# An attention kernel's first and last microseconds: 24 drains ahead of VectorE's program, the sums checked before the last finishing steps, the last store from ScalarE's queue

## The chip, the cores and the metric

The kernel runs on one core of a Trainium2 chip. The metric is the device time of one execution in microseconds. Before the change it is 1798.63 us, the median of three runs (1798.06 to 1798.91).

## The reference

The input `x` has 32 images of 256 channels and 32 x 32 positions. It is group-normalised in 32 groups, projected to queries, keys and values, and goes through attention with 8 heads of 32 channels over the 1024 positions. A position attends only to earlier ones (`tril(..., -1)`); the first one attends to nothing. The result is added to `x`.

```
q, k, v = heads(q_w @ gn(x) + q_b), heads(kv_w @ gn(x) + kv_b)
scores  = where(mask == 0, -10000, q @ k.T / sqrt(32))
attn    = where(mask == 0, 0, softmax(scores))
out     = x + heads_back(attn @ v)
```

## The kernel before

The kernel is one long, unrolled program for each engine, `unshifted()`, followed by a fallback, `shifted()`, under a runtime condition. The first takes the exponentials of the scores without taking their maximum off; the fallback does the same work with the maximum taken off, in loops, and is there for inputs whose sums of exponentials leave the range from 1e-20 to 1e20. With the inputs of this case it is never entered.

In `unshifted()` the order on every engine is written out by hand (`tc.manual_schedule`). The work is cut into visits, 12 for an image and 384 in all. In a visit TensorE computes scores (line 310), products of exponentials and values (line 421) and projections for the next image (line 169); ScalarE takes the exponentials (lines 392 and 396); GpSimd masks the diagonal blocks (line 338); VectorE adds exponentials up over the keys (line 439). Sums of one image are folded by DMAs, inverted and used in `finish` some visits later: `finish` multiplies the products by the inverse sums (line 543), adds the bias of the values and `x` (line 545) and sends the result from SyncE's queue (line 551).

At the start VectorE takes statistics of the first image (line 184). They feed the first products of TensorE that are not mere warming up (line 169), and so everything behind them.

The last image has no later visits to hide in. Its sums are made by TensorE (line 473), inverted by `invert_here` (lines 530 to 533), and its last quarter is finished in `end_last`, in two halves of 256 columns. For each half VectorE transposes the sums, inverts them and spreads them (`invert_here`); then for each half it runs `finish`, whose store goes out as soon as the half is done. Behind that `end_last` looks whether all sums were in range:

```
check(inv_last.rearrange("p n k -> p (n k)"), 1.0 / SUM_MAX, 1.0 / SUM_MIN)
nc.vector.tensor_reduce(worst, in_range, AX.X, ALU.min)
nc.tensor.matmul(pc[0:1, 0:1], lhsT=worst, rhs=ones, start=True, stop=True)
nc.vector.tensor_scalar(outside, pc[0:1, 0:1], -1.0, float(P), ALU.mult, ALU.add)
```

`check` is lines 494 and 495, the reduction line 567, the matmul line 569 and the last VectorE step line 571. The number `outside`, rows that were out of range, is then loaded into a register of each of the five engines (line 901), with an assertion on SyncE that it lies from 0 to 128. Each engine compares it with zero and jumps over its part of `shifted()` (line 902), which lies in its program between the branch and the end. At the end SyncE waits for one semaphore after another, those of all DMA queues and engines (line 925; called its ladder below, each wait a rung), and a barrier of all engines closes the program.

Of the kernel before, what the change touches and what calls it, by code (L numbers as in the profile page):

```python
# [10 lines left out]
I32 = mybir.dt.int32  # L11
AF = mybir.ActivationFunctionType
ALU = mybir.AluOpType
# [4 lines left out]
P = 128  # L18
HD = 32
CPG = 8  # L20
HALF = 512
# [11 lines left out]
def tile_norm_attention_residual(  # L33
# [19 lines left out]
    nc = tc.nc  # L53
    B, C, H, W = x.shape
# [7 lines left out]
    const = ctx.enter_context(tc.tile_pool(name="const", bufs=1))  # L62

    x_in = x.rearrange("b (g p) h w -> b p g (h w)", p=P)
    x_out = out.rearrange("b (g p) h w -> b p g (h w)", p=P)
# [15 lines left out]
        out=avg, in_=avg, pattern=[[-CPG, P // CPG], [0, CPG]],  # L81
# [3 lines left out]
        out=avg, in_=avg, pattern=[[CPG, P // CPG], [0, CPG]],  # L85
# [13 lines left out]
    def unshifted():  # L99
# [9 lines left out]
        def load(b):  # L109
            width = S if b else HALF  # L110
            for g in range(NG):
                for at in range(0, S, width):
                    load_part(b, g, slice(at, at + width))
# [12 lines left out]
        def misc(name):  # L126
            return ps_m.tile([P, HALF], F32, tag="misc", name=name)


        def load_weights(junk):  # L130

            arrived = tc.alloc_semaphore("arrived")
            nc.scalar.activation(junk, live["x", 0][:, 0, HALF : HALF + 1], AF.Identity)
            nc.scalar.sem_inc(arrived, 1)
            nc.sync.wait_ge(arrived, 1)
            for n, w in enumerate((q_w, kv_w[0:C], kv_w[C : 2 * C])):
                live["wn", n] = epool.tile([P, 4, HALFBANK], F32, tag="eh", bufs=3, name=f"wn_{n}")[:, :NG, :C]
                nc.sync.dma_start(out=live["wn", n], in_=w.rearrange("(o p) c -> p o c", p=P))
            nc.sync.dma_start(out=qk_bias[:, 0, :], in_=q_b.rearrange("(g p) -> p g", p=P))
            nc.sync.dma_start(out=qk_bias[:, 1, :], in_=kv_b[0:C].rearrange("(g p) -> p g", p=P))  # L140
            nc.sync.dma_start(out=v_bias_col, in_=kv_b[C : 2 * C].rearrange("(g p) -> p g", p=P))
# [32 lines left out]
        def blocks(tokens, s, turned=False):  # L174

            of = tokens.rearrange("p (n s t) -> p n s t", s=2, t=P)[:, :, s, :]
            return of[:, :, ::-1] if turned else of
# [315 lines left out]
        def check(rows, least, most):  # L493
            nc.vector.scalar_tensor_tensor(in_range, rows, least, in_range, ALU.is_ge, ALU.mult)
            nc.vector.scalar_tensor_tensor(in_range, rows, most, in_range, ALU.is_le, ALU.mult)
# [27 lines left out]
        def invert_here(b, n, within=slice(0, HALF)):  # L523


            if ("rb", b) not in live:
                live["rb", b] = work.tile([P, 4, HALF], F32, tag="folded", bufs=1, name="rb_last")
            k = (within.stop - within.start) // HD
            turned = small.tile([P, HALF], F32, tag="turned", bufs=1, name=f"turned_{b}_{n}_{within.start}")[:, : k * HD]
            nc.vector.transpose(turned, live["den", n][:, within])  # L530
            inv = inv_last[:, n, within.start // HD : within.stop // HD]
            nc.vector.reciprocal(inv, turned.rearrange("p (k r) -> p k r", r=HD)[:, :, 0])
            nc.vector.transpose(  # L533
                live["rb", b][:, n, within].rearrange("p (k r) -> p k r", r=HD),
                inv.unsqueeze(2).broadcast_to([P, k, HD]),
            )

        def finish(b, n, within=slice(0, HALF), later=None):
            g, hf = divmod(n, NH)
            cols = slice(hf * HALF + within.start, hf * HALF + within.stop)  # L540
            num, rb, xt = live["num", b, n], live["rb", b][:, n, within], live["x", b]
            num = num[:, within]
            nc.vector.tensor_mul(num, num, rb)  # L543
            for s in range(2):
                nc.vector.scalar_tensor_tensor(  # L545
                    blocks(rb, s), blocks(num, s, s == 1), v_bias_col[:, g : g + 1], blocks(xt[:, g, cols], s),
                    ALU.add, ALU.add,
                )
            if cols.start == 0:
                nc.vector.tensor_copy(rb[:, 0:1], xt[:, g, 0:1])  # L550
            send = lambda: nc.sync.dma_start(out=x_out[b, :, g, cols], in_=rb)
            if later is None:
                send()
            else:
                later(send)

        def end_last(b):

            both = [slice(c * HALFBANK, (c + 1) * HALFBANK) for c in range(2)]
            for part in both:  # L560
                invert_here(b, 3, part)
            for part in both:
                finish(b, 3, part)

            check(inv_last.rearrange("p n k -> p (n k)"), 1.0 / SUM_MAX, 1.0 / SUM_MIN)
            worst = const.tile([P, 1], F32, name="worst")
            nc.vector.tensor_reduce(worst, in_range, AX.X, ALU.min)
            pc = misc("pc")
            nc.tensor.matmul(pc[0:1, 0:1], lhsT=worst, rhs=ones, start=True, stop=True)
            outside = const.tile([1, 1], I32, name="outside")  # L570
            nc.vector.tensor_scalar(outside, pc[0:1, 0:1], -1.0, float(P), ALU.mult, ALU.add)
            return outside

# [53 lines left out]
        def when(i, f, where=at):  # L629
            where.setdefault(i, []).append(f)  # L630
# [19 lines left out]
        SPREAD = (2, 2, 3, 4)  # L650
        FINISH = (N + 13, N + 13, N + 14, N + 16)
        every = range(4)

        with tc.manual_schedule(engines={ENG.PE, ENG.Activation, ENG.DVE, ENG.Pool, ENG.SP}):

# [1 line left out]
            junk = small.tile([P, 1], F32, tag="most", name="junk")  # L657
            nc.scalar.activation(junk, ones, AF.Exp)
            load_weights(junk)
            if B > 1:  # L660
                load(1)
            keep_busy(16)
# [30 lines left out]
            for b in range(B):  # L693
# [4 lines left out]
                if b >= 2:  # L698
                    for n in range(NG * NH):
                        cols = slice(n % NH * HALF, (n % NH + 1) * HALF)  # L700
# [5 lines left out]
                if not last:  # L706
# [16 lines left out]
                    for n in every:  # L723
                        v = first + (N + 9 + n // 2 if late else FINISH[n])
                        later = None if late else lambda send, first=first, v=v, n=n: when(*((first + 2 * N + 4, send) if n < 2 else (v + 1, send, after)))
                        when(v, lambda b=b, n=n, later=later: finish(b, n, later=later), after)
                else:
                    when(first + 3, lambda: sums(0, SUMMED[1], False), after)
                    when(first + 7, lambda: sums(1, SUMMED[5], False), after)
                    when(first + 9, lambda: sums(2, SUMMED[7], False), after)  # L730
                    when(first + 8, lambda b=b: invert_here(b, 0))
                    when(first + 9, lambda b=b: finish(b, 0))
                    when(first + 8, lambda b=b: invert_here(b, 1))
                    when(first + 8, lambda b=b: finish(b, 1))
                    when(first + 10, lambda b=b: invert_here(b, 2))
                    when(first + 11, lambda b=b: finish(b, 2), after)
            for i in range(B * N + 1):
# [4 lines left out]
                b, v = divmod(i - 1, N)  # L742
# [12 lines left out]
                for f in after.pop(i, ()):  # L755
                    f()
            assert not at and not between and not after
            outside = end_last(B - 1)
        for p in reversed(pools):
            p.release()  # L760
        for ins in nc.cur_bb.bb.instructions:
            if "TilePoolBoundary op=release" in ins.concise():
                tc.declare_no_dep(ins, group="first", reason="exponentials behind them are waited for")
        return outside

    def shifted():


        with ExitStack() as inner:
# [34 lines left out]
            with tc.For_i(0, B, 1) as b:  # L804
# [92 lines left out]
                    out=x_out[bass.ds(b, 1)].rearrange("o p g s -> p (o g) s"), in_=y.rearrange("p (g s) -> p g s", g=NG)  # L897
                )

    outside = unshifted()  # L900
    again = nc.values_load(outside[0:1, 0:1], min_val=0, max_val=P)
    with tc.If(again > 0):
        shifted()


# [23 lines left out]
```

## Time and profile before

| | us |
|---|---|
| median of three runs | 1798.63 |
| the profiled execution | 1799.27 |
| its span | 1797.57 |
| TensorE busy in the span | 1784.9 |
| VectorE busy | 1674.2 |
| ScalarE busy | 1456.0 |
| GpSimd busy | 879.7 |

In the profile PE is TensorE, DVE VectorE, ACT ScalarE, POOL GpSimd and SP SyncE. A q behind the name means the engine's sequencer, which also issues its DMAs. L551 is line 551 of the kernel before. Times in a timeline count from the start of the span. The granted clock of TensorE is 0.998 of full speed. Loading a register, branching, waiting for semaphores and issuing DMAs do not count as busy time, and the chain of work that the page follows back from the end starts at the last instruction that does.

### The profile page before, as it was taken

Reading aid. Unit: us, or ns where it says so; the run is one execution under the profiler, and the core shown is the slowest. Engines: PE = TensorE matmul, PEld = TensorE weight load, DVE = VectorE, ACT = ScalarE, POOL = GpSimd, SP = SyncE. Lnnn points to the kernel's source line nnn. Section 1 sums busy time; section 2 is a strip of 40 time slices with the busy share of each in tenths; the row PEclk is TensorE's granted clock in tenths of the full one; section 3 lists DMA queues with packets and bytes.
Section 4 is the critical chain, followed back from the end, with each engine's and each line's share of the span. In section 5 each row is a group of like instructions: output and inputs, shape, how many; then the busy total and the mean of one; then the engine's idle time right before and its main releaser. Section 6 shows DMA issues by size and latency. Waiting matters only on the chain.

```text
span 1797.6 us, 81793 instructions
## 1 busy us (share of the span) xinstructions
PE 1784.9 (99%) x37036; PEld 948.4 (53%) x37036; DVE 1674.2 (93%) x1830; ACT 1456.0 (81%) x1986; POOL 879.7 (49%) x902
## 2 busy tenths in 40 slices
PE   9999999999999999999999999999999999999997
PEld 5555555555555555555555555555555555555553
DVE  4689999999999999999999999999999999999998
ACT  6888878888778888788887888887888878888774
POOL 2345554554545455445545455554454544554541
PEclk9999999999999999999999999999999999999999
DMA  2566766766667667677676777666766666776663
GB/s 69 105 121 132 134 132 129 149 141 138 125 130 149 145 131 133 133 136 146 137 138 130 126 147 146 133 134 133 141 143 134 134 133 127 150 141 140 121 118 88
DMA packets 86819, 236.77 MB, mean 132 GB/s; under 512 B 21313, under 2 KB 22337, under 8 KB 70593
## 3 DMA queue, kind: packets, MB, share of 16 engines
q0 software_dynamic: 15872, 97.53, 39.8%
q1 hardware_dynamic: 70592, 133.96, 25.7%
q8 instruction: 290, 4.75, 1.2%
q14 instruction: 65, 0.52, 0.1%
HBM read 66.85 MB, written 34.57 MB: 56 GB/s over the span
## 4 chain that ended last, share of the span: by engine, by line
PE 99%; DVE 0%; ACT 0%; issue 0%; POOL 0%; POOLq 0%
PE sT L310 31%; PE acc L421 28%; PE pp L169 26%; PE ppv L169 13%; PE pd L473 1%; PE busy L155 0%; ACT e L396 0%; PE pv L169 0%; PE pm L169 0%; DVE rb_last L545 0%; PE wt L148 0%; ACT eh L392 0%; DVE rb_last L533 0%; DVE turned L530 0%; DVE acc L543 0%
## 5 line engine op out<-in xcount | busy, mean ns | idle before, releaser
L338 POOL TENSOR_SCALAR_AFFINE_SELECT diagonal<-eh 128x512 f32<-128x512 f32 x512 | 633.4, 1260 | 842.0 <-ACT eh L392 841.6
L396 ACT ACTIVATE e<-sT 128x1024 f32<-128x1024 f32 x768 | 744.3, 1022 | 249.8 <-PE sT L310 227.2
L439 DVE TENSOR_TENSOR e<-e,e 128x1024 f32<-128x1024 f32 x314 | 575.3, 1832 | 24.5 <-ACT v L274 3.2
L310 PE MATMUL sT<-q,k 32*64 32x128 f32 (+2 forms) x18432 | 579.4, 372 | 0.3 <-issue 0.2
L310 PEld LDWEIGHTS sT<-q,k 32*64 32x64 f32 x18432 | 395.0, 131 | 189.3 <-PE sT L310 69.6
L169 PE MATMUL pp<-xn,wT 128*32 128x512 f32 x4096 | 492.3, 598 | 0.0
L421 PE MATMUL acc<-e,v 128*32 128x512 f32 (+3 forms) x4608 | 401.0, 450 | 0.0
L392 ACT ACTIVATE eh<-sT 128x768 f32<-128x768 f32 (+1 forms) x384 | 341.7, 890 | 0.0
L421 PEld LDWEIGHTS acc<-e,v 128*32 128x32 f32 x4608 | 149.2, 110 | 261.5 <-issue 238.9
L169 PE MATMUL ppv<-wT,xn 128*32 128x256 f32 x4096 | 247.5, 382 | 0.0
L439 DVE TENSOR_TENSOR diagonal<-diagonal,e 128x1536 f32<-128x1536 f32 x126 | 195.1, 1548 | 17.1 <-PE acc L421 9.2
L169 PEld LDWEIGHTS pp<-xn,wT 128*32 128x32 f32 x4096 | 107.1, 109 | 195.8 <-issue 164.0
L439 DVE TENSOR_TENSOR e<-e,eh 128x1024 f32<-128x1024 f32 x126 | 163.9, 1301 | 6.5
L421 PEld LDWEIGHTS acc<-diagonal,v 128*32 128x32 f32 x4096 | 121.1, 110 | 87.6 <-issue 75.7
L439 DVE TENSOR_TENSOR e<-e,diagonal 128x2048 f32<-128x2048 f32 x63 | 144.2, 2289 | 19.3 <-POOL diagonal L338 19.2
L169 PEld LDWEIGHTS ppv<-wT,xn 128*32 128x32 f32 x4096 | 120.1, 109 | 79.7 <-issue 7.0
L421 PE MATMUL acc<-diagonal,v 128*32 128x128 f32 x4096 | 158.8, 273 | 0.0
L243 ACT ACTIVATE xn<-x,shift,rstd 128x256 f32<-128x256 f32 x248 | 136.8, 608 | 1.0 <-POOL shift L226 0.9
L543 DVE TENSOR_TENSOR num<-num,rb 128x512 f32<-128x512 f32 x124 | 122.8, 991 | 0.4 <-DMA rb<-inverses 0.4
L545 DVE SCALAR_TENSOR_TENSOR rb<-num,v_bias_col,x 128x256 f32<-128x256 f32 x248 | 117.5, 515 | 4.4
L452 POOL DMA_DIRECT2D e<-e x124 | 102.1, 823 | 38.6 <-issue 38.6
L452 POOL DMA_DIRECT2D diagonal<-diagonal x124 | 103.2, 832 | 5.8 <-issue 4.9
(80 smaller groups left out, 983.8 us busy)
## 6 DMA issues: line engine op xcount, KB each, us to landing
x<-in_x_dram SPq DMA_DIRECT2D x124, 256.0 KB, 3.7
diagonal<-diagonal POOLq DMA_DIRECT2D x62, 512.0 KB, 5.6
e<-e POOLq DMA_DIRECT2D x62, 512.0 KB, 6.1
rb<-inverses SPq DMA_DIRECT2D x124, 256.0 KB, 4.3
out_dram<-rb SPq DMA_DIRECT2D x124, 256.0 KB, 4.9
diagonal<-diagonal POOLq DMA_DIRECT2D x62, 256.0 KB, 4.6
folded<-diagonal SPq DMA_DIRECT2D x62, 256.0 KB, 5.3
e<-e POOLq DMA_DIRECT2D x62, 256.0 KB, 5.0
```

Source lines behind the costliest of these rows:

```text
L169: nc.tensor.matmul(out[part], lhsT=lhsT[:, part], rhs=rhs, start=start, stop=stop, skip_group_check=True)
L243: nc.scalar.activation(to, of, AF.Identity, bias=live["shift", b][:, g : g + 1], scale=rstd)
L310: return nc.tensor.matmul(bank[c : c + KEYS, cols], lhsT=live["k", b, g][rows, kb * P + c : kb * P + c + KEYS], rhs=live["q", b, g][rows, ...
L338: nc.gpsimd.affine_select(out=square[:, :, place + s * P : place + (s + 1) * P], in_=raw[:, :, (1 - s) * KEYS : (3 - s) * KEYS], pattern=[ ...
L392: exp = nc.scalar.activation(eh.rearrange("p (n bank) q -> p bank n q", n=2)[:, :, :, :narrow], short[:, :, :, :narrow], AF.Exp)
L396: nc.scalar.activation(e[:, 2 * a : 2 * a + 2, :wide], pairs[a][:, :, :wide], AF.Exp)
L421: nc.tensor.matmul(acc[HD * j : HD * (j + 1), of], lhsT=live["v", b][:, kb, h * HD : (h + 1) * HD], rhs=e[:, j, :], start=first, stop=last ...
L439: nc.vector.tensor_add(to, to, tile_of(b, g, at))
L452: nc.gpsimd.dma_start(out=total[:rows], in_=total[rows : 2 * rows], accum_op=ALU.add)
L473: nc.tensor.matmul(pd[HD * j : HD * (j + 1), of], lhsT=pick, rhs=e[:, j, :], start=start, stop=stop, skip_group_check=True,)
L543: nc.vector.tensor_mul(num, num, rb)
L545: nc.vector.scalar_tensor_tensor(blocks(rb, s), blocks(num, s, s == 1), v_bias_col[:, g : g + 1], blocks(xt[:, g, cols], s), ALU.add, ALU.add,
```

## The change

- Ahead of its first instruction of `unshifted()`, VectorE's program gets 24 drains, which wait until the engine has nothing in flight and do nothing else.
- In `end_last`, `check`, the reduction and the matmul come before both calls of `finish` instead of behind them.
- The count is no longer made from the matmul's result by VectorE (128 minus it): ScalarE copies the result itself into an integer, `inside`, the number of rows in range. The condition becomes `rows < P` instead of `again > 0`.
- The store of the second half is sent from ScalarE's queue, that of the first half from SyncE's as before.
- The assertion on the loaded value is left out.

```
-        def finish(b, n, within=slice(0, HALF), later=None):
+        def finish(b, n, within=slice(0, HALF), later=None, queue=nc.sync):
...
-            send = lambda: nc.sync.dma_start(out=x_out[b, :, g, cols], in_=rb)
+            send = lambda: queue.dma_start(out=x_out[b, :, g, cols], in_=rb)
...
                 invert_here(b, 3, part)
-            for part in both:
-                finish(b, 3, part)
-
             check(inv_last.rearrange("p n k -> p (n k)"), 1.0 / SUM_MAX, 1.0 / SUM_MIN)
...
             nc.tensor.matmul(pc[0:1, 0:1], lhsT=worst, rhs=ones, start=True, stop=True)
-            outside = const.tile([1, 1], I32, name="outside")
-            nc.vector.tensor_scalar(outside, pc[0:1, 0:1], -1.0, float(P), ALU.mult, ALU.add)
-            return outside
+            inside = const.tile([1, 1], I32, name="inside")
+            nc.scalar.copy(inside, pc[0:1, 0:1])
+            for part in both:
+                finish(b, 3, part, queue=nc.sync if part.start == 0 else nc.scalar)
+            return inside
...
+        ALIGN = 24
...
             load_weights(junk)
+            for _ in range(ALIGN):
+                nc.vector.drain()
...
-    again = nc.values_load(outside[0:1, 0:1], min_val=0, max_val=P)
-    with tc.If(again > 0):
+    rows = nc.values_load(
+        inside[0:1, 0:1], min_val=0, max_val=P, skip_runtime_bounds_check_because="it counts rows of one tile"
+    )
+    with tc.If(rows < P):
         shifted()
```

More of the change, by code (lines that the diff above doesn't have):

```diff
@@ L757, in unshifted @@
             assert not at and not between and not after
-            outside = end_last(B - 1)
+            inside = end_last(B - 1)
         for p in reversed(pools):
@@ L763, in unshifted @@
                 tc.declare_no_dep(ins, group="first", reason="exponentials behind them are waited for")
-        return outside
+        return inside
     def shifted():
@@ L898, in shifted @@
                 )
-    outside = unshifted()
-    again = nc.values_load(outside[0:1, 0:1], min_val=0, max_val=P)
-    with tc.If(again > 0):
+    inside = unshifted()
+    rows = nc.values_load(
+        inside[0:1, 0:1], min_val=0, max_val=P, skip_runtime_bounds_check_because="it counts rows of one tile"
+    )
+    with tc.If(rows < P):
         shifted()
```

## The prediction

> **What bounds the kernel now.** I read the page first: the row of busy times and the chain that ended last.
>
> ```profile
> PE 1784.9 (99%) x37036; PEld 948.4 (53%) x37036; DVE 1674.2 (93%) x1830; ACT 1456.0 (81%) x1986; POOL 879.7 (49%) x902
> ...
> PE 99%; DVE 0%; ACT 0%; issue 0%; POOL 0%; POOLq 0%
> ```
>
> TensorE is the bound, and the change leaves its 37,036 matmuls in place and in order. So only the two ends, where TensorE isn't the bound, can move. The second view is VectorE's timeline of the last 12 us (start, duration, what; idle time before it in brackets).
>
> ```profile
> 1787.98 0.45 DVE L533 STREAM_TRANSPOSE rb_last<-inv_last 128x256 f32<-128x256 f32 x1
> 1788.35 0.40 DVE L543 TENSOR_TENSOR acc<-acc,rb_last 128x256 f32<-128x256 f32 x1
> 1788.79 0.61 DVE L545 SCALAR_TENSOR_TENSOR rb_last<-acc,v_bias_col,x 128x128 f32<-128x128 f32 x2
> 1789.43 0.43 DVE L543 TENSOR_TENSOR acc<-acc,rb_last 128x256 f32<-128x256 f32 x1
> 1789.90 0.61 DVE L545 SCALAR_TENSOR_TENSOR rb_last<-acc,v_bias_col,x 128x128 f32<-128x128 f32 x2
> 1790.43 0.21 DVE L494 SCALAR_TENSOR_TENSOR in_range<-inv_last,in_range 128x64 f32<-128x64 f32 x1
> ...
> 1790.94 0.22 DVE L567 TENSOR_REDUCE worst<-in_range 128x1 f32<-128x64 f32 x1
> 1791.53 0.15 DVE L571 TENSOR_SCALAR outside<-pc 1x1 int32<-1x1 f32 x1 [0.37 <-PE pc L569]
> ```
>
> The last arithmetic ends at 1791.68, yet the span ends at 1797.57: 5.9 us hold no work at all, and the page's chain stops before them. The third view, the instructions of line 902 (the `If`), shows who is late there (durations in ns, then first start in us).
>
> ```profile
> L902 ACTq COMPARE_BRANCH  x1: 50/50/50, 1792.2 to 1792.2; - x1
> L902 POOLq COMPARE_BRANCH  x1: 45/45/45, 1792.3 to 1792.3; - x1
> ...
> L902 DVEq COMPARE_BRANCH  x1: 72/72/72, 1792.3 to 1792.3; - x1
> ...
> L902 ACTq EVENT_SEMAPHORE  x1: 17/17/17, 1792.7 to 1792.7; - x1
> ...
> L902 POOLq EVENT_SEMAPHORE  x1: 17/17/17, 1792.8 to 1792.8; - x1
> L902 DVEq EVENT_SEMAPHORE  x1: 21/21/21, 1796.5 to 1796.5; - x1
> ```
>
> Every engine jumps over the unused `shifted()`. ScalarE and GpSimd go on 0.4 us after their branch; VectorE goes on at 1796.47, 4.07 us after its branch ended at 1792.40, with nothing else to wait for. SyncE, which collects all semaphores before the last barrier, stands still for it; this is from its own waits (us in total, times, longest):
>
> ```profile
> SPq L925 <- DVEq L902: 2.6, 1, 2.6
> ```
>
> From there to the end it is 1.05 us (1796.52 to 1797.57).
>
> **Why VectorE is late.** The page's DMA queues show how instructions come in.
>
> ```profile
> q8 instruction: 290, 4.75, 1.2%
> q14 instruction: 65, 0.52, 0.1%
> ```
>
> Queue 14 brings 8 KB a packet. In the trace's records one such packet starts each time VectorE has begun 63 to 66 instructions more than a multiple of 128: at 341.79 us it stood at 447, at 429.01 at 578, at 603.48 at 832, at 1719.87 at 2497. So a page is 128 instructions, and crossing into one fetches the next. VectorE's last page began at about 2497 and ended at 2624; the fetched next one ended at about 2752. Its branch is its 2616th record, and the built program skips 137 instructions on VectorE, so the jump lands at 2754, just past both pages. For ScalarE (pages at 61 past a multiple of 128, branch 2725, 131 skipped) and SyncE (80 past, 1071, 126) the same count lands inside, and these were the quick ones.
>
> [...]
>
> **The change, part by part.** All on the profiled execution, 1799.27 us with a span of 1797.57; its 1.7 us around the span I leave alone. The median of the runs is 0.64 lower, and the same difference is taken from it.
>
> *The pad.* 24 drains added, one VectorE instruction (L571) gone: the branch is its 2639th record, in the page that starts near 2625; the target, 2777, lies in the next one (2753 to 2880), fetched since 14 instructions before the branch, at the first last-bank transpose (1786.94), 4.3 us ahead. Even if that fetch needs the whole 4.07 us it is there by 1791.0. Page starts are known to about 2 instructions, which 14 covers. VectorE's jump then costs 0.4 us, as ScalarE's. Alone, with the old order, this would let SyncE go through its ladder without stopping: it reached VectorE's semaphore at 1793.90, ends 1.05 + 0.02 us later, 1794.97, a gain of 2.6.
>
> The drains themselves stand ahead of VectorE's first statistics. The cover is a wait:
>
> ```profile
> DVE st L184 <- DMA x<-in_x_dram: 4.3, 2, 3.5
> ```
>
> VectorE is released at 0.74 and idles until 3.49, and again 0.77 before the second one: 3.5 us can be filled, 0.146 a drain. A drain on an empty VectorE is in the closing barrier:
>
> ```profile
> L925 POOLq DRAIN  x3: 46/105/463, 1792.9 to 1797.3; - x3
> ...
> L925 DVEq DRAIN  x2: 10/14/17, 1796.6 to 1797.0; - x2
> ```
>
> 10 to 17 ns each, 0.11 us from the instruction before to the drain's start: 24 x 0.11 = 2.6 us, inside the cover. I take 0. Without cover it would be 2.6 straight onto TensorE's chain; the far end is GpSimd's 463 ns.
>
> *Checks ahead of the finishing steps.* L494, L495 and L567 take from 1790.43 to 1791.16, 0.73, less the 0.08 by which neighbours overlap: 0.65. They now begin at 1788.35, and both finishing steps slide by 0.65: the last one ends at 1791.16 instead of 1790.51, its store is issued at 1791.19 instead of 1790.54, the first half's at 1790.08. So this part costs the last store 0.65, and takes the count off the end.
>
> *ScalarE's copy and the test.* The reduction ends at 1789.08; matmul to its end 0.33, then a small PSUM copy (L192 took 0.17): the count is ready near 1789.6. Every engine's load of it (0.47 to 0.54) waits for that alone: GpSimd and TensorE jump long before the end. VectorE's load stands behind its last finishing step: at worst 1791.16 + 0.54 + 0.07 + 0.4 = 1792.2. ScalarE's stands behind the last store, which waits for VectorE: 1791.19 + 0.33 + 0.5 + 0.1 + 0.4 = 1792.5. ScalarE has had nothing to do since 1784.2, so nothing else is queued there.
>
> *The store on ScalarE's queue.*
>
> ```profile
> out_dram<-rb_last SPq DMA_DIRECT2D x2, 128.0 KB, 1.8
> ```
>
> Issued 1790.54, landed 1792.36: 1.82. No ScalarE issue is in the trace. Bounds: SyncE's price from the one side (nothing extra; SyncE already issued 0.03 after VectorE's end, so no gain is to be had), GpSimd's from the other (0.82 an issue against 0.33, so +0.5, and landings of 4.6 for 256 KB, so up to +2.8). I take SyncE's, the nearest. Landing at 1793.01.
>
> *No assertion.* SyncE's register operation (0.19) and assert (0.03) delayed its branch by 0.27. Now SyncE loads after the first half's store (1790.43), jumps, and starts its ladder near 1791.5; the eighth rung, the last store's semaphore, is reached at 1792.2 and holds it until 1793.01. The assertion is covered by 0.8 us: 0.
>
> *Sum.* The last store's landing takes VectorE's place. Released at 1793.04, two more rungs at 0.06 bring SyncE to VectorE's semaphore, and 1.05 remain: 1794.21. The span ends 3.36 us sooner: 1798.63 - 3.36 = 1795.27.
>
> **The rivals.**
>
> *A, forecast:* as summed. Landing 0.3 either way, ScalarE's first issue up to 0.5 dear, and medians that a spread of 0.85 over three runs leaves loose by about 0.5: 1794.4 to 1796.2.
>
> *B, the jump still misses* (page starts misread, or the page not kept). VectorE's sequencer may take its load while the last finishing step still runs (the step's two halves already overlap by 0.08), so its branch ends between 1791.3 and 1791.85; 4.07 later and 1.1 on, the end is at 1796.5 to 1797.0, a gain of 0.6 to 1.1: 1797.5 to 1798.0. For it: the old target missed the window by only about two instructions, as counted by me. Against: the shift is 23.
>
> *C, slower: the drains outlast their cover.* TensorE's first real product (pm, L169) waits for VectorE's statistics, and all of TensorE's chain behind it. At GpSimd's 463 ns, 24 drains take 11.1 us, 7.6 past the cover: 1795.27 + 7.6 = 1802.9. It beats A's gain from 0.29 us a drain, and is slower by over 0.2% from 0.44. VectorE's own 10 to 17 ns speak against.
>
> *D, the new queue is dear.* At GpSimd's prices, +0.5 and +2.8, the end comes at 1797.5, and the gain all but goes: 1795.8 to 1798.6. Stores of SyncE at 1.8 to 2.0 speak against.
>
> **How the numbers follow.** A 0.82, B 0.08, D 0.06, C 0.04. 0.2%, about what a measurement of this kernel can tell from no change, is 3.6 us, or 1795.03: A's centre is 0.24 short of it and its spread several times that, so A gives faster a little over half: 0.42. Same has the rest of A, 0.40, with B and most of D: 0.53. Slower, C and an unlucky remainder: 0.05. The range takes A whole and part of D, leaving out B, C and the rest of D: 1794.2 to 1797.2.
>
> **What would show it.** Right: VectorE's line 902 semaphore 0.3 to 0.5 us after its branch; SyncE's longest closing wait on a store instead of on VectorE; last store issued by ScalarE near 1791.2 and landing 1.8 later; first statistics still at about 3.5 us; span near 1794.2. Wrong: a VectorE gap of 4 us left (B), first statistics past 4.3 (C), a ScalarE landing over 2.3 us (D), or a TensorE stretch between 20 and 1780 us that differs by more than 1 us, which nothing here foresees.

## The result, and the profile after

| | before | after |
|---|---|---|
| median of 22 runs each, us | 1798.64 (1797.85 to 1801.20) | 1796.22 (1795.26 to 1797.52) |
| the profiled execution | 1799.27 | 1796.62 |
| its span | 1797.57 | 1794.92 |

The ratio is 0.9987, with an interval of 0.9981 to 0.9992: 2.4 us sooner, 0.13%. That is inside the 0.2% that the prediction counted as no change, 0.95 above its 1795.27 and at the upper edge of forecast A (1794.4 to 1796.2).

The page's row of busy times is as before but for small shifts, and the instruction queue has one packet fewer; the new line is ScalarE's queue.

```profile
PE 1784.7 (99%) x37036; PEld 948.8 (53%) x37036; DVE 1674.7 (93%) x1829; ACT 1457.1 (81%) x1987; POOL 879.8 (49%) x902
...
q14 instruction: 64, 0.52, 0.1%
q10 hardware_dynamic: 144, 0.13, 0.0%
```

VectorE's timeline of the end (start, duration, what) has the checks ahead of both finishing steps:

```profile
1787.85 0.45 DVE L533 STREAM_TRANSPOSE rb_last<-inv_last 128x256 f32<-128x256 f32 x1
...
1788.70 0.22 DVE L564 TENSOR_REDUCE worst<-in_range 128x1 f32<-128x64 f32 x1
1788.83 0.42 DVE L543 TENSOR_TENSOR acc<-acc,rb_last 128x256 f32<-128x256 f32 x1
...
1790.40 0.61 DVE L545 SCALAR_TENSOR_TENSOR rb_last<-acc,v_bias_col,x 128x128 f32<-128x128 f32 x2
```

From the start of that last transpose to the end of the span before took 9.58 us (1787.98 to 1797.57), and takes 7.07 now (1787.85 to 1794.92). This stretch is called the tail below. It holds 2.52 of the span's 2.65 us; the transpose itself starts 0.13 sooner.

The lines of the `If` (now 906; durations in ns, then first and last start) show that VectorE is no longer late. It goes on at 1791.81, 0.49 us after its branch ended at 1791.32; before it was 4.07.

```profile
L906 DVEq COMPARE_BRANCH  x1: 72/72/72, 1791.2 to 1791.2; - x1
L906 DVEq EVENT_SEMAPHORE  x1: 21/21/21, 1791.8 to 1791.8; - x1
```

SyncE's closing wait is on the store now, and the landings (median us from issue) show what it waited for:

```profile
SPq L929 <- DMA out_dram<-rb_last: 1.7, 1, 1.7
```

```profile
out_dram<-rb_last SPq DMA_DIRECT2D x1, 128.0 KB, 1.9
out_dram<-rb_last ACTq DMA_DIRECT2D x1, 128.0 KB, 2.7
```

The last store was issued at 1791.05 and landed at 1793.71: 2.66 us instead of 1.82. The trace has 16 landing records for a store. 14 of this one's were there by 1793.03, where the prediction had all of it (1793.01); the last two came at 1793.62 and 1793.71. Before, all 16 came from 1792.16 to 1792.36. While it ran, instruction packets came in at 1791.20, 1791.31 (the 16 KB one, 1.14 us long), 1791.94, 1792.43 and 1793.06. The records name no engine for them; that the engines that had just jumped were fetching is the author's reading and not shown.

### The profile page after: what moved, and what is told of

It is laid out like the page before. It is cut to its first block, busy times and chain, and to the rows that moved or that the text cites. A ratio compares the mean times of both kernels' runs of the same rounds, so it can differ in the third digit from the quotient of the medians.

```text
span 1794.9 us, 81815 instructions
## 1 busy us (share of the span) xinstructions
PE 1784.7 (99%) x37036; PEld 948.8 (53%) x37036; DVE 1674.7 (93%) x1829; ACT 1457.1 (81%) x1987; POOL 879.8 (49%) x902
## 4 chain that ended last, share of the span: by engine, by line
PE 99%; DMA 0%; ACT 0%; DVE 0%; issue 0%; SPq 0%; DVEq 0%; ACTq 0%
PE sT L310 31%; PE acc L421 28%; PE pp L169 26%; PE ppv L169 13%; PE pd L473 1%; DMA x<-in_x_dram 0%; DMA wn<-in_L_conv_kv_w_dram 0%; ACT e L396 0%; PE pv L169 0%; PE pm L169 0%; DVE rb_last L545 0%; ACT eh L392 0%; DVE rb_last L533 0%; SPq L138 0%; DVE turned L530 0%
```

## The experiments

Three questions. Does VectorE's pad bring the gain, as the prediction has it? Did the last store land late because ScalarE's queue is dear (rival D), or because the instruction packets behind the jumps run beside it? And is the assertion free? A median, of 11 runs unless said otherwise, is set against that of the kernel before in the same batch. "VectorE gap" is the time from the end of its branch to its next step.

**The pad alone.** The kernel before, with the 24 drains only.

```
             load_weights(junk)
+            for _ in range(24):
+                nc.vector.drain()
```

> The kernel before with the 24 drains alone. Theory 1 (VectorE's jump left the fetched pages, and the pad brings its target back into them): VectorE goes on 0.4 to 0.6 us after its branch instead of 4.07, SyncE's 2.6 us wait for it is gone, and the time is 2.6 us under before, near 1796.0. Theory 2 (the gain came from taking the count off the end, and the pad does nothing): VectorE still takes 4 us, the time is that of before, 1798.6.

Measured: 1798.6 against 1798.6, ratio 1.0 (0.9991 to 1.0009). VectorE's gap closed, as the lines of the `If` show, yet nothing was gained:

```profile
L904 POOLq COMPARE_BRANCH  x1: 45/45/45, 1793.3 to 1793.3; - x1
...
L904 DVEq COMPARE_BRANCH  x1: 72/72/72, 1793.3 to 1793.3; - x1
...
L904 DVEq EVENT_SEMAPHORE  x1: 21/21/21, 1793.9 to 1793.9; - x1
```

The lines of the closing barrier show who is late instead. SyncE begins its part at 1795.1; GpSimd's first step in it starts at 1797.5, 4.21 us after its branch ended at 1793.33.

```profile
L927 POOLq EVENT_SEMAPHORE  x4: 17/17/17, 1797.5 to 1798.2; - x4
...
L927 POOLq DRAIN  x3: 46/105/463, 1793.8 to 1798.1; - x3
...
L927 SPq DRAIN  x3: 7/7/7, 1795.1 to 1797.8; - x3
```

GpSimd is quick over its jump (it goes on 0.43 after the branch, and the drain behind that comes at 1793.8) and slow behind it. In the kernel before, this was covered:

```profile
L925 POOLq EVENT_SEMAPHORE  x4: 17/17/17, 1796.8 to 1797.5; - x4
```

That 1796.77 comes 0.03 after SyncE, which VectorE had held until then, so the row can't tell whether GpSimd was ready. With the 4.21 measured here it would have been, from 1792.32 on, near 1796.5: 0.2 ahead of VectorE's delay. Two engines were late by nearly the same time. SyncE's own waits don't help either: they put the new 2.5 us down to TensorE, whose drain in the barrier had come at 1794.0.

```profile
SPq L927 <- PEq L927: 3.1, 2, 2.5
```

**The order without the pad.** The changed kernel with `ALIGN = 0`: by the prediction's counting VectorE's jump lands at 2753.

```
-        ALIGN = 24
+        ALIGN = 0
```

> The changed kernel without drains. VectorE's program is one instruction shorter than before's, so its jump lands at 2753 by my count, on the edge of the fetched pages (known to about 2). Theory 1, target outside: VectorE goes on 4.07 us after its branch, near 1795.4, and the time is 0.6 to 1.1 us under before, 1797.5 to 1798.0. Theory 1, target just inside: VectorE goes on after 0.4 to 0.6, and the time is the changed kernel's, 1796.2. Theory 2: the changed kernel's time, with VectorE's 4 us gone or hidden.

Measured: 1796.54 against 1798.6, ratio 0.9989 (0.998 to 0.9998). The jump is late again, but it comes earlier and costs less: the branch ends at 1790.49 and VectorE goes on at 1793.74, 3.24 us later. SyncE waits 1.4 for the store and then 1.0 for VectorE.

```profile
L906 DVEq COMPARE_BRANCH  x1: 72/72/72, 1790.4 to 1790.4; - x1
...
L906 DVEq EVENT_SEMAPHORE  x1: 21/21/21, 1793.7 to 1793.7; - x1
```

```profile
SPq L929 <- DMA out_dram<-rb_last: 1.4, 1, 1.4
SPq L929 <- DVEq L906: 1.0, 1, 1.0
```

So the rest of the change brings 2.06 of the 2.4 us without any drain; the tail is 7.81, against 7.07 with the pad and 9.58 before. Of these 1.77 us, 0.95 come from the branch, which ends 3.47 us after the start of the last transpose instead of 4.42, and 0.82 from a wait behind it of 3.24 instead of 4.07; from VectorE's step to the end it is 1.10 in both. Why this wait is shorter is open. The medians with and without the pad differ by 0.3, within the intervals.

**The last store from SyncE.** The changed kernel with both halves on SyncE's queue.

```
-                finish(b, 3, part, queue=nc.sync if part.start == 0 else nc.scalar)
+                finish(b, 3, part, queue=nc.sync)
```

> The changed kernel with the last store sent from SyncE's queue again. In the changed kernel this store took 2.66 us from issue to landing, two of its sixteen parts landing 0.8 after the others. Theory Q (ScalarE's queue is dear in its first use): it lands after 1.8 us, and as SyncE's jump moves behind it to about 1792, SyncE ends its ladder near 1793.2 and the span is 0.5 to 0.8 shorter. Theory F (instruction pages fetched after the early jumps of TensorE, GpSimd and VectorE go through the same DMA engines): it still lands after 2.3 to 2.7 us, and the time is within 0.4 of the changed kernel's.

Measured: 1796.05 against 1798.6, 0.9988 (0.9979 to 0.9997). The last store is as late from SyncE: issued 1790.57, 14 parts by 1792.35, the last at 1793.14, 2.57 us.

**ScalarE's queue in the old order.** The kernel before, with only the last store moved.

```
...
-            send = lambda: nc.sync.dma_start(out=x_out[b, :, g, cols], in_=rb)
+            send = lambda: queue.dma_start(out=x_out[b, :, g, cols], in_=rb)
...
-                finish(b, 3, part)
+                finish(b, 3, part, queue=nc.sync if part.start == 0 else nc.scalar)
```

> The kernel before with the last store sent from ScalarE's queue and nothing else. All jumps come after this store, as before. Theory Q: it takes 2.4 to 2.8 us from issue to landing. Theory F: 1.8 to 1.9 us, all sixteen parts together. VectorE's late jump, 4.07 us, still sets the end, so the time is that of before within 0.4 by both.

Measured: 1798.72 against 1798.6, 1.0001 (0.9992 to 1.001). All parts landed together, 1.86 us after the issue:

```profile
out_dram<-rb_last SPq DMA_DIRECT2D x1, 128.0 KB, 1.8
out_dram<-rb_last ACTq DMA_DIRECT2D x1, 128.0 KB, 1.9
```

In this profile the queue isn't dear, and rival D falls. What goes with late parts is that the engines jump while the store runs. In all eight kernels with the old order, here and below, the last store had landed when the first instruction packet behind the jumps came: 1.81 to 1.86 us. In the six with the new order it had not: 2.00, 2.06, 2.41, 2.57, 2.66 and 3.50. Sharing time is not enough by itself: the first half's stores of the changed kernel and of the one without the pad still ran when the first packets started, and landed in 1.86 and 1.85. That these packets and the store meet in the same DMA engines was not shown: the records used here don't say which engine carried which packet.

**Both pads, GpSimd's between visits.** The pad alone, and 48 drains on GpSimd as well, one in each of the visits 24 to 71, to move the rest of its program by 48 (5 runs each, here and in the next two).

```
...
                 for f in after.pop(i, ()):
                     f()
+                if 24 <= i < 72:
+                    nc.gpsimd.drain()
```

> The kernel before with the 24 drains on VectorE and 48 drains on GpSimd, one a visit in visits 24 to 71. With the 24 alone, VectorE's jump took 0.49 us, SyncE came to the barrier at 1795.15, and GpSimd's first barrier step came at 1797.54, 4.2 us after its branch. Theory G (GpSimd's jump lands on the last instructions of its fetched pages and the step after them must be fetched; behind VectorE's 4.07 us this was hidden): with its program moved by 48, GpSimd stands ready and answers SyncE within 0.1 us; the end falls by 2.4 us, the time is near 1796.1. Theory 2 (GpSimd needs these 4 us for something else, its closing drain for one): GpSimd still comes 4.2 us after its branch, time 1798.6.

Measured: 1827.46 against 1798.67, 1.016 (1.0147 to 1.0174). The tail did what was expected (6.98), but 29 us were lost in the middle. The table by windows (window, its length, busy time of PE, PEld, DVE, ACT, POOL, granted clock, DMA share, GB/s) shows TensorE idle there for 19.6 us of 1,760, where before it idled for 0.67; the matmuls' busy time over the whole span grew as well, from 1784.9 to 1798.4. First the kernel before, then this one:

```profile
20.00:1780.00 1760.00, 1759.33 (x36684) 932.37 (x36676) 1655.64 (x1779) 1443.87 (x1968) 875.78 (x885) 1.00 0.67 132
```

```profile
20.00:1780.00 1760.00, 1740.42 (x36040) 917.57 (x36036) 1618.47 (x1736) 1420.83 (x1939) 844.81 (x875) 1.00 0.67 130
```

So a drain on GpSimd between visits held up the work behind it, by about 0.6 us each (29 over 48). What GpSimd had running at each of them wasn't taken apart. That a drain waits for running work shows in the profile before, where GpSimd has 31 of its own (line 451): they took 2.57 to 4.02 us, and each ended 0.33 to 0.74 us after the two masks (line 338) that ran beside it. Two more kernels of that batch had the same loop and lost the same. The first has no assertion:

```
-    again = nc.values_load(outside[0:1, 0:1], min_val=0, max_val=P)
+    again = nc.values_load(
+        outside[0:1, 0:1], min_val=0, max_val=P, skip_runtime_bounds_check_because="it counts rows of one tile"
+    )
```

> The same with both pads, and without the assertion; the order of before, the count from VectorE. By theory G SyncE's way from the load to its last step is all that is left, so the 0.27 us of the assertion count in full: 1795.8. It would equal the changed kernel with no change of order and no second queue. By theory 2: 1798.6.

Measured: 1827.38, 1.0159 (1.0145 to 1.0173), tail 6.64. The second is the changed kernel with this loop and a cheaper count: GpSimd makes the two comparisons, TensorE and ScalarE sum them, VectorE does nothing for them. The number counted is now that of all marks in range, and the condition compares it with `3 * P * ROW`.

```
+            marks = [in_range]
+            for tag, limit, op in (("rows", 1.0 / SUM_MAX, ALU.is_ge), ("inv", 1.0 / SUM_MIN, ALU.is_le)):
+                marks.append(small.tile([P, ROW], F32, tag=tag, name=f"mark_{tag}"))
+                nc.gpsimd.tensor_scalar(marks[-1], inv_last.rearrange("p n k -> p (n k)"), limit, 1.0, op, ALU.mult)
...
+            for n, mark in enumerate(marks):
+                nc.tensor.matmul(pc[0:1, 0:ROW], lhsT=ones, rhs=mark, start=n == 0, stop=n == 2)
...
+            nc.scalar.activation(in_range[0:1, :], pc[0:1, 0:ROW], AF.Identity, accum_out=total)
+            nc.scalar.copy(inside, total)
...
+    with tc.If(rows < 3 * P * ROW):
```

> The changed kernel with both pads and the two comparisons moved from VectorE to GpSimd, TensorE summing the marks of all rows and columns, ScalarE summing those 64 sums and converting. VectorE's last store is issued 0.65 us sooner after the last inverses than in the changed kernel. If it lands after 1.8 us the span ends 5.6 us after the start of the last L533, if instruction pages meet it and it takes 2.6, 6.4, against 7.07 in the changed kernel: 0.7 to 1.5 us under it, 1794.7 to 1795.5. If GpSimd's comparisons take over 2 us the count is late and it gains nothing.

Measured: 1826.83, 1.0157 (1.0143 to 1.017), tail 5.83. The whole times of these three say nothing on the pads; their tails do, and are what the next batch rests on.

**The assertion kept.** The changed kernel with it.

```
     rows = nc.values_load(
-        inside[0:1, 0:1], min_val=0, max_val=P, skip_runtime_bounds_check_because="it counts rows of one tile"
+        inside[0:1, 0:1], min_val=0, max_val=P
     )
```

> The changed kernel with the assertion kept. The prediction's step: SyncE's 0.27 us are covered by its wait for the last store, in the changed kernel 1.7 us long, so the time is the changed kernel's within 0.3. A rival: the assertion's longer program moves SyncE's pages and makes its jump late, 3 to 4 us more.

Measured: 1796.87 against 1798.67, 0.999 (0.9981 to 0.9999), 0.65 above the changed kernel, more than the 0.3 that was expected, but the intervals overlap. SyncE was held by stores: both landed late in this profile (3.92 and 3.50 us), and it stood at the first half's until 1794.48. Its load and branch now stood ahead of the first half's store, which was issued 2.46 us after the last transpose instead of 2.08. Its own jump was quick (0.46). What the assertion costs in the new order stays open, between nothing and about 0.7 us.

**Both pads, all drains at the start.** 34 drains on GpSimd behind VectorE's 24 in the program, in a stretch in which GpSimd has nothing to do (in the profile before from 2.45 to 9.58 us).

```
+            for _ in range(24):
+                nc.vector.drain()
+            for _ in range(34):
+                nc.gpsimd.drain()
```

> The kernel before with 24 drains on VectorE and 34 on GpSimd, both at the start, where GpSimd is idle from 2.5 to 9.6 us (drains between visits cost 29 us, and are avoided here). Theory G: both jumps stay inside fetched pages, from the start of the last L533 to the end it is 6.98 us as in the run with drains between visits, against 9.58 before: 2.6 less, 1796.0. Theory 2: no gain, 1798.6.

Measured: 1796.14 against 1798.45, 0.9986 (0.9977 to 0.9995), tail 6.98. Both engines are in time, the stores land in 1.83 and 1.81, and the barrier starts with GpSimd ready:

```profile
L929 POOLq EVENT_SEMAPHORE  x4: 17/17/17, 1793.6 to 1794.3; - x4
...
L929 SPq DRAIN  x3: 7/7/7, 1793.6 to 1793.9; - x3
```

**GpSimd's pad alone.**

```
+            for _ in range(34):
+                nc.gpsimd.drain()
```

> The kernel before with 34 drains on GpSimd alone. Theory G: GpSimd stands ready early, but VectorE still goes on 4 us after its branch and sets the end: the time of before, 1798.6, within 0.4. A rival (GpSimd alone was the bound): 2.4 us less.

Measured: 1798.46 against 1798.45, 1.0002 (0.9993 to 1.0011). VectorE's gap is 4.11 and holds SyncE for 2.68, the longest of its closing steps:

```profile
L927 SPq EVENT_SEMAPHORE  x14: 17/28/2679, 1792.4 to 1796.6; - x14
```

With it the square is closed: neither pad 1798.6 and 1798.45 in the two batches, VectorE's 1798.6, GpSimd's 1798.46, both 1796.14. In the old order each pad is worth nothing without the other.

**Both pads, no assertion.** The kernel before with 24 and 34 drains at the start, and the loaded value without its assertion, by the edit shown above for that.

> Both pads at the start and no assertion, otherwise before. With drains between visits the last L533 to the end was 6.64 us, 0.34 less than with the assertion: 1795.7. The assertion counts here because SyncE's own way is the last.

Measured: 1795.77 against 1798.45, 0.9984 (0.9975 to 0.9993), tail 6.64. In the old order the assertion delays the tail by 0.34, because SyncE is then the last.

**The best version.** The changed kernel with the cheaper count and both pads at the start.

> The changed kernel with the comparisons on GpSimd, the sums by TensorE and ScalarE, and both pads at the start. With drains between visits the last L533 to the end was 5.83 us, against 7.07 in the changed kernel: 1.2 under it, 1795.0; if the last store meets instruction pages as in the changed kernel (2.66 us instead of the 2.06 of that run), 0.6 under it, 1795.6.

Measured: 1795.02 (1794.54 to 1795.66) against 1798.45, 0.9981 (0.9972 to 0.999), tail 5.77: the fastest kernel of this case. GpSimd's two comparisons run beside VectorE's transposes, and the finishing steps don't slide:

```profile
1786.93 0.46 POOL L565 TENSOR_SCALAR mark_rows<-inv_last 128x64 f32<-128x64 f32 x1 [7.31 <-DVE inv_last L532]
1787.47 0.43 POOL L565 TENSOR_SCALAR mark_inv<-inv_last 128x64 f32<-128x64 f32 x1
```

**All runs together.** If only the tail moves, a median should be that of the kernel before in its batch, less what the tail lost against 9.58. The three kernels with drains between visits are not in the table: they lost their time in the middle.

| kernel | tail, us | median by that | measured |
|---|---|---|---|
| VectorE's pad alone | 9.34 | 1798.4 | 1798.6 |
| ScalarE's queue alone | 9.17 | 1798.2 | 1798.7 |
| GpSimd's pad alone | 9.62 | 1798.5 | 1798.5 |
| changed, no pad | 7.81 | 1796.8 | 1796.5 |
| changed, assertion kept | 7.91 | 1797.0 | 1796.9 |
| changed | 7.07 | 1796.1 | 1796.2 |
| both pads at the start | 6.98 | 1795.9 | 1796.1 |
| changed, last store from SyncE | 6.96 | 1796.0 | 1796.1 |
| both pads, no assertion | 6.64 | 1795.5 | 1795.8 |
| best version | 5.77 | 1794.6 | 1795.0 |

The tails, each from one profile, account for every median to about 0.5 us.

## Why the prediction was right, and where it was wrong

**Where the time is.** Right: TensorE's stretch did not move (busy for 1759.3 us before and 1759.5 after, of the 1760 from 20 to 1780), and the last 6 us without arithmetic were the whole matter.

**Why VectorE is late.** Right as far as it goes: a branch 20 to 24 instructions later closed the gap, from 4.07 to 0.49, in all ten kernels with the pad, and in the four without it the gap was 3.24 to 4.11. The page starts were not known as well as the text said. Over the whole trace before, the 8 KB packets that keep step with VectorE come at 56 to 71 past a multiple of 128, not at 63 to 66. They show where VectorE stood when they started, and not what they brought: that entering a page fetches the next is the text's reading. And in the changed kernel a packet at 1779.49, with VectorE at its 2609th instruction, came 16 before the start it gave, 2625. It comes at 2609 in all ten kernels with VectorE's pad and in none of the four without, so it goes with VectorE's program; why it comes early is open. If it brought the page, the page was there sooner than the sum had it, which does the sum no harm.

**The pad: the step that failed.** "Alone, with the old order, ... a gain of 2.6" measured 0. It went along SyncE's ladder, took 1.05 us from VectorE's semaphore to the end, and took it that every other engine would be at the barrier by then. For GpSimd the text went by its quick jump, and counted no pages. In the trace before 8 KB packets start with GpSimd 65 to 68 past a multiple of 128, once 71; its branch is its 1191st record and 153 are skipped. So by the text's way of counting its target, 1345, is among the last two or three instructions of two pages, and the next page would have to come in behind it. The records fit this, though they show no page: of the steps behind the jump the first two, 1345 and 1346, come in time in the pad alone and the third, 1347, is the late one; and in all seven kernels with drains on GpSimd an 8 KB packet starts with GpSimd at its 1219th to 1221st record, one page of 128 ahead of that place. The question "what is late next" was put to the store alone.

**The drains.** Taken at 0, and that holds, with a price smaller than the sum had:

```profile
L661 DVEq DRAIN  x24: 10/10/10, 0.8 to 1.8; - x24
```

24 drains took 0.92 us, 0.040 from one to the next and not 0.11, while VectorE waited for x until 3.88. Rival C falls. The first statistics come 0.39 later than in the profile before; but that is x, which came as late, at 3.82 to 3.85, in the three other kernels without drains on VectorE. The second ones start anywhere from 4.21 to 5.58 over the kernels of this case, and the last transpose started sooner.

**Checks ahead of the finishing steps.** Predicted 0.65 for the last store; from the start of the last transpose to the issue it is 3.19 instead of 2.55: 0.64.

**ScalarE's copy.** Predicted 1789.6; it ran from 1789.29 to 1789.44. VectorE's load began at 1790.42, while its last finishing step still ran, so its branch ended at 1791.32, and not at the 1791.8 behind the bound of 1792.2. This is the early end that the prediction kept for rival B.

**What the part did that the text missed.** Taking the count off the end also moved GpSimd's jump, to 1790.08 from 1792.32. Its slow stretch behind the jump was over by 1794.12 at the latest, 0.03 after SyncE:

```profile
L929 POOLq EVENT_SEMAPHORE  x4: 17/17/17, 1794.1 to 1794.8; - x4
...
L929 SPq DRAIN  x3: 7/7/7, 1794.0 to 1794.3; - x3
```

The end itself came by the way of the sum: 1.21 us behind the last store's landing, where the sum had 1.20. But the gain came for another reason than the text gave: without the pad the rest of the change still took most of it (2.06 of 2.4), by taking both jumps forward against the last transpose, GpSimd's by 2.1 us and VectorE's by 0.95. Which part of the change did that is read from the traces; no run has the order and the copy alone. That its earlier jump also covered GpSimd's slow stretch is luck: the prediction did not know of the stretch. GpSimd may have been close to setting the end itself. Had the store landed at 1793.01, SyncE would have reached the barrier near 1793.4, and a GpSimd that needs 4.04 us would have come to it at the same 1794.12. Whether it was ready sooner, no run tells: the least bound without its pad is 3.95, in the kernel with the last store from SyncE. In all five kernels in which a store is SyncE's last long wait, two of them with GpSimd's pad, the end follows the landing by the same 1.21.

**The store: the term mis-sized.** 1.82 was taken for the landing, 2.66 came, +0.84. The prediction's bound of +0.5 and +2.8 held, for another cause than its queue. By its own sign (a landing over 2.3) D would have been read as right; the store alone on that queue, at 1.86, and the same lateness from SyncE's queue, 2.57, show that it was not. In the span: 0.84 for the landing, less 0.14 because the store was issued at 1791.05 and not at 1791.19, is 0.70, and 1794.21 + 0.70 is 1794.91, against the 1794.92 of the profile. Of the 0.95 us between the predicted and the measured median, the other 0.24 is that the profiled executions stood 0.64 above their median before and 0.40 after.

**The assertion.** Taken at 0 here, not settled more closely than 0.7 us. In the old order it is worth 0.34 once both engines are in time.

**Rival B.** Its case was made by leaving the pad out. It gave a gain of 0.6 to 1.1; 2.06 was measured, 1.77 of it in the tail of the profile. The branch ended 3.47 us after the last transpose's start, as its early end had it, but the wait behind it was 3.24 and not 4.07.

## What to carry to other kernels

When one engine is late at a barrier, the trace can't show a second one that is late by a little less; price each engine's way to it by itself, for here two were late by nearly the same time (4.07 and 4.21 us behind their branches), and mending either alone gave nothing (1798.6 and 1798.46, against 1796.14 for both). A jump near the end of a program was cheaper here when it came early (2.06 us sooner with no pad at all): load the value that it depends on as soon as it exists, so that the wait behind the jump lies beside the last arithmetic and stores. And price a store at the end with the traffic that will then run beside it (2.66 us here), not as it was when it ran alone (1.82).

## What the runs showed of the hardware

- An engine can be late without a late jump. GpSimd went on 0.42 to 0.43 us after its branch, and came to its first barrier step 4.21 us after the branch in the pad alone (1797.5, SyncE's at 1795.1); with 34 drains ahead it was in time (both at 1793.6). That it goes away with the shift is shown; that it is the crossing into the next page was not shown, and is the author's reading of the count above.
- In the four kernels without its pad VectorE went on 4.07, 4.11, 3.66 and 3.24 us after its branch, with the pad 0.49. In the three of these with the old order four 8 KB instruction packets started 0.9 to 1.3 us after VectorE's branch and lasted 0.3 to 0.6; VectorE went on 1.9 to 2.4 us after the last of these had ended, which stays unexplained.
- The last store of 128 KB, where it was still running when these packets came, landed in 2.0 to 3.5 us instead of 1.8, by two late parts out of 16, four in the slowest. Of the four first-half stores that ran beside them one took 3.9, the others 1.8 to 1.9.
- 48 drains on GpSimd between visits cost 29 us; 34 at the start, most of them 0.061 us apart, cost nothing that a median shows.
